# A four-layer graph network on one core: GpSimd's score tiles get a second ALU stage, and the planner a shorter price for them

## The chip, the cores and the metric

One Trainium2 chip, one of its cores. The metric is the device time of one execution in microseconds (us); the kernel before took 5291.05 us (median of three runs, 5291.04 to 5301.35). The engines are TensorE (PE), VectorE (DVE), ScalarE (ACT), GpSimd (POOL) and SyncE (SP, which here only issues DMAs). Each works through its own list of instructions in order[...].

## The reference

The input `x` is 64 graphs of 256 nodes with 128 features, `adj` one 256 x 256 matrix for all of them, everything in float32. Four layers follow each other; each normalizes, clips at zero, and adds its result to `x`:

```python
h = jnp.maximum(_layernorm(x), 0.0); x = x + _L0(h, adj, adj, ...)   # 5 steps of a gated recurrence
h = jnp.maximum(_layernorm(x), 0.0); x = x + _L1(h, adj, adj, ...)   # Chebyshev hops of order 2
h = jnp.maximum(_layernorm(x), 0.0); x = x + _L2(h, adj, ...)        # product, rows scaled to length 1
h = jnp.maximum(_layernorm(x), 0.0); x = x + _L3(h, adj, ...)        # additive attention
```

The change lies in the last layer. Its scores need every pair of nodes (i, j) and every one of 256 features e:

```python
pre = s1[:, :, None, :] + s2[:, None, :, :] + b_lin
h = jnp.where(pre >= 0, pre, ALPHA * pre)          # ALPHA = 0.2
e = jnp.einsum('bije,e->bij', h, a) + bias
out = sigmoid(einsum('bij,bjf->bif', softmax(e, axis=2), x))
```

## The kernel before, in words

**Tiling.** Two graphs make a pair; there are 32 pairs. For each pair a *front* computes layers 0 to 2 and the two terms `s1` and `s2` of layer 3, as a chain of steps on PE, ACT, DVE and POOL. Then come the *scores* of the pair. Features lie on the 128 partitions in two halves (half 0: features 0 to 127, half 1: the others). A score tile `rl` holds 4 rows i, both graphs and all 256 j of one half (128 x 2048 numbers). 64 tiles per half and pair make 4096 tiles in all. Up to a part that is linear in `pre` and is added later (`lin`), leaky ReLU is a ReLU, and the ReLU of `s1 + s2` is `s1` minus the minimum of `s1` and `-s2`; what is constant along j drops out of the softmax, so a tile can be made in either form, and the weights `win` (for a ReLU) or `win_n` (for a minimum) carry the sign.

**Three makers of tiles** (`work_on_tile`):
- DVE makes half 0 only, one minimum of 128 x 2048 per tile (line 737), reading `s1a` from SBUF and `-s2` from a PSUM bank.
- ACT makes half 1 in 8 ReLU activations of 128 x 256 (line 750) from a PSUM copy of `s2n`, and takes a tile of half 0 (from `s2c` in SBUF) when DVE has fallen two tiles behind (`half`, `LAG`).
- POOL makes half 1 only, in 8 `tensor_scalar` instructions of 128 x 256 (line 757): the minimum of `s2n` with one column of `s1b`, a scalar for each partition. Two of these are one part of a tile, and a tile has four parts.

PE then multiplies each tile with `win` or `win_n` into one of two score banks (`score`, line 794: four column groups of 32, which the trace shows as 8 matmuls, two passes each). After 64 tiles of both halves a block of 128 rows i is done, and a *tail* makes the softmax and the output: `lin` is added on POOL (line 648), the exponential on ACT (line 656), and `o = 0.5 o + 0.5` on POOL with an immediate `mult` and an immediate `add` (line 686), followed by the addition of `x3` (line 687).

**The order.** It is planned while the program is built. `clock[engine]` is the planner's time for each engine; `ran(engine, us, ...)` books a piece of work with a price written in the code, and the loop at the end takes the engine that is earliest and gives it, of what is ready by the plan, a step of a tail first, then of a front, then a tile. The prices for tiles are 2.2 us on DVE, 1.43 us (half 1) or 1.6 us (half 0) for 4 activations on ACT, 1.8 us for two instructions on POOL, and 0.86 us for the matmuls of a tile. `in_order` then fixes each engine's list. The plan thus decides who makes which tile and where each tile stands in PE's list; the chip keeps the list, whatever the pieces really take. Thirteen `rl` buffers exist, of which DVE may hold 8, ACT 3 and POOL 2 (`MOST`); a buffer comes free when PE has multiplied its tile. A front's pace is set by the number of tiles scored (`chain_ready`), not by time, so fronts advance with the scores; the last front is through when 3920 of 4096 tiles are scored.

Of the kernel before, what the change touches and what calls it, by code (L numbers as in the profile page):

```python
# [10 lines left out]
OP = mybir.AluOpType  # L11
# [6 lines left out]
LN_EPS = 1e-5  # L18
NORM_EPS = 1e-12
ALPHA = 0.2  # L20
PE, DVE, ACT, POOL = ENGINES = (mybir.EngineType.PE, mybir.EngineType.DVE, mybir.EngineType.Activation, mybir.EngineType.Pool)
SLOTS = 64

# [2 lines left out]
def kernel(  # L26
# [50 lines left out]
    nc = tc.nc  # L77
# [22 lines left out]
    def ran(engine, us, *after):  # L100
        start = max(clock[engine], 0.0, *after)
        if engine == ACT:
            behind[0] = max(0.0, behind[0] - (start - clock[ACT])) + 0.024 * us
        clock[engine] = start + us
        return clock[engine] + SEEN[engine] + (behind[0] if engine == ACT else 0.0)
# [19 lines left out]
    last, done = {}, [0]  # L125
# [123 lines left out]
    def other_constants():  # L249
# [29 lines left out]
        for k in range(NE):  # L279
            nc.vector.tensor_scalar(win[:, k, 31:32], acol[:, k:k + 1], 1.0 - ALPHA, None, op0=OP.mult)  # L280
            nc.vector.tensor_scalar(win_n[:, k, 31:32], acol[:, k:k + 1], ALPHA - 1.0, None, op0=OP.mult)
            nc.vector.tensor_scalar(a_rep[:, k, :], a_rep[:, k, :], acol[:, k:k + 1], None, op0=OP.mult)
# [7 lines left out]
        yield DVE, t  # L290
        nc.vector.tensor_scalar(g2, b[0][:, 0:P], ALPHA, None, op0=OP.mult)
        t = ran(DVE, 0.25, t)
# [413 lines left out]
    def where(n):  # L706
        return n // SLOTS, n % SLOTS // 32, n % 32

    def half(e):

        return 0 if e == DVE or e == ACT and following[0] <= following[1] - LAG else 1

    def tile_ready(e):

        if e in begun:
            return 0.0
        n = following[half(e)]
        if n >= NSLOT or n // SLOTS not in READY or held[e] == MOST[e] or not tiles:
            return None
        return max(READY[n // SLOTS]["since"][half(e)], min(t[1] for t in tiles))  # L720

    def work_on_tile(e):
        if e not in begun:
            k = half(e)
            tiles.sort(key=lambda t: t[1])
            begun[e] = [following[k], k, *tiles.pop(0), 0]
            following[k] += 1
            held[e] += 1
        n, k, t, free, part = begun[e]
        p, ic, r = where(n)  # L730
        ops = READY[p]
        i0 = ic * P + r
        since = max(ops["since"][k], free)
        if e == DVE:
            whole = [P, 4, NB, N]
            rows = ops["s1"][0][:, :, i0:i0 + 97:32].rearrange("p b g -> p g b").unsqueeze(3)
            nc.vector.tensor_tensor(t, rows.to_broadcast(whole), ops["s2a"].unsqueeze(1).to_broadcast(whole), op=OP.min)  # L737
            done = ran(DVE, 2.2, since)
            t_s2v[p % 2] = done
            parts = 1  # L740
        elif e == ACT:
            if k and "s2p" not in ops:
                ops["s2p"] = s2p
                nc.scalar.copy(s2p, ops["s2n"])
                ran(ACT, COPY, since)
            parts = 2
            for g in (2 * part, 2 * part + 1):
                for b in range(NB):
                    i = i0 + g * 32
                    nc.scalar.activation(t[:, g, b, :], (s2p if k else ops["s2c"])[:, b, :], AF.Relu,  # L750
                                         bias=ops["s1"][k][:, b, i:i + 1], scale=-1.0)
            done = ran(ACT, 1.43 if k else 1.6, since)
        else:
            parts = 4
            for b in range(NB):
                i = i0 + part * 32
                nc.gpsimd.tensor_scalar(t[:, part, b, :], ops["s2n"][:, b, :], ops["s1"][1][:, b, i:i + 1], None, op0=OP.min)  # L757
            done = ran(POOL, 1.8, since)
        begun[e][4] += 1
        if part + 1 == parts:  # L760
            del begun[e]
            made.append((done, n, k, t, e))
# [55 lines left out]
    def chain_ready(key, e):  # L818

        engine, since, bank, gate = (*CHAINS[key][1], 0, None)[:4] if len(CHAINS[key][1]) < 4 else CHAINS[key][1]  # L820
        if engine != e or bank and not spare or gate and not gate():
            return None
        if not isinstance(key, tuple) and 0 < key < NPAIR and spare:

            due = STEPS_OF_FRONT * (scored[0] / (2 * SLOTS) - (key - 2)) / SPREAD
            if CHAINS[key][2] > due + AHEAD:
                return None
        return max(since, min(b[1] for b in spare)) if bank else since
# [15 lines left out]
    while scored[0] < 2 * NSLOT or CHAINS:  # L844
# [4 lines left out]
        for key in CHAINS:  # L849
            since = chain_ready(key, e)  # L850
# [6 lines left out]
        else:  # L857
            since = tile_ready(e)
# [3 lines left out]
        if ready:  # L862
            _, (rank, *_), what = min(ready, key=lambda x: x[1])
            if rank < 2:
                advance(what)
            elif e == PE:
                score(what)
            else:
                work_on_tile(e)
            in_order()  # L870
            now[e] = max(now[e], clock[e])
        else:
            later = [x[0] for x in todo] + [t for t in now.values() if t > now[e]]
            now[e] = min(later) if later else now[e] + 1.0
# [31 lines left out]
```

## Time and profile before

| what | value |
|---|---|
| runs of the kernel | 5301.35, 5291.04, 5291.05 us; median 5291.05 us |
| span of the profiled execution | 5298.6 us; the page gives it no other time, and of the runs the one of 5301.35 us is the nearest above it |
| granted TensorE clock | full, but for the first and the last stretch (0.96 and 0.90) |
| first score matmul | 123.3 us |
| last front's last ACT step (`s1a`, line 628) | starts at 5097.5 us |
| last score tile's matmuls | start at 5285.8 us |
| DMA | 7 GB/s on the mean |

How to read it: the page gives busy time as the union of an engine's instructions. The mean duration of a group can be longer than the distance between two starts, since instructions of an engine overlap at their ends; how fast a row really goes is read from a run of them in the timeline, or from its busy time divided by its count. PE's ends are modelled, so its busy share says little by itself. "Idle before" a row and the name after the arrow say how long the engine stood still and what ended that. In the table by stretches each engine's busy time is followed by the number of its instructions.

### The profile page before, as it was taken

How to read it: one execution, taken by the hardware profiler on the slowest of the kernel's cores; microseconds unless marked ns; L12 is line 12 of the kernel's file. 1: busy time of each engine (PE TensorE's matmuls, PEld its weight loads, DVE VectorE, ACT ScalarE, POOL GpSimd, SP SyncE). 2: the span in 40 equal slices, each digit the busy share in tenths (PEclk: the TensorE clock that was granted, in tenths of full speed). 3: DMA queues.
4: the chain of work that ended last, by engine and by line, in shares of the span. 5: the costliest groups of instructions: out<-in, count | busy, mean ns of one | idle time of the engine just before them, and what ended most of it. 6: DMA issues, size and time to landing. Idle time of an engine off the chain costs nothing. (4 is left out here: it accounts for less than half of the span.)

```text
span 5298.6 us, 138351 instructions
## 1 busy us (share of the span) xinstructions
PE 5215.3 (98%) x56085; PEld 1855.4 (35%) x56085; DVE 5194.6 (98%) x4198; ACT 5093.4 (96%) x13353; POOL 5126.0 (97%) x5894
## 2 busy tenths in 40 slices
PE   7999999999999999999999999999999999999998
PEld 3333333333333333333333333333333333333322
DVE  3999999999999999999999999999999999999999
ACT  4999999999999999999999999999999999999999
POOL 2999999999999999999999999999999999999998
PEclk9999999999999999999999999999999999999999
DMA  0000000000000000000000000000000000000000
GB/s 20 7 8 5 8 7 6 8 5 8 8 5 8 7 6 8 7 6 8 5 8 8 5 8 6 6 8 7 6 8 5 8 7 6 8 5 6 6 5 4
DMA packets 60338, 37.44 MB, mean 7 GB/s; under 512 B 4528, under 2 KB 59696, under 8 KB 59696
## 3 DMA queue, kind: packets, MB, share of 16 engines
q1 hardware_dynamic: 58976, 28.59, 2.3%
q8 instruction: 438, 7.18, 0.6%
q14 instruction: 204, 1.67, 0.1%
q10 hardware_dynamic: 720, 0.00, 0.0%
HBM read 18.09 MB, written 10.49 MB: 5 GB/s over the span
## 5 line engine op out<-in xcount | busy, mean ns | idle before, releaser
L757 POOL TENSOR_SCALAR rl<-s2n,s1b 128x256 f32<-128x256 f32 x5064 | 4565.0, 943 | 11.4 <-ACT s1b L619 8.9
L737 DVE TENSOR_TENSOR rl<-s1a,bank 128x2048 f32<-128x2048 f32 x2046 | 4545.1, 2276 | 10.6 <-ACT s1a L628 10.6
L750 ACT ACTIVATE rl<-bank,s1b 128x256 f32<-128x256 f32 x11320 | 4538.6, 923 | 2.5 <-PE bank L794 1.3
L794 PE MATMUL bank<-rl,win_n 128*32 128x512 f32 x21432 | 2646.6, 593 | 32.0 <-DVE rl L737 29.7
L794 PE MATMUL bank<-rl,win 128*32 128x512 f32 x11336 | 1493.5, 593 | 0.0
L794 PEld LDWEIGHTS bank<-rl,win_n 128*32 128x32 f32 x21432 | 678.2, 110 | 1513.5 <-issue 1242.2
L794 PEld LDWEIGHTS bank<-rl,win 128*32 128x32 f32 x11336 | 363.8, 110 | 745.6 <-issue 621.4
L305 PE MATMUL bank<-mT,wts 128*32 128x512 f32 x2560 | 332.9, 592 | 0.0
L305 PE MATMUL bank<-adj_t,h 128*32 128x256 f32 x5120 | 309.4, 382 | 3.6 <-ACT h L492 3.3
L473 POOL TENSOR_TENSOR d<-d,hT 128x512 f32<-128x512 f32 x155 | 203.3, 1311 | 53.2 <-ACT d L469 53.2
L305 PEld LDWEIGHTS bank<-adj_t,h 128*32 128x32 f32 x5120 | 165.4, 111 | 178.6 <-issue 63.1
L376 ACT ACTIVATE h<-x,mv 128x128 f32<-128x128 f32 x384 | 171.8, 631 | 45.3 <-POOL mv L372 45.2
L382 ACT COPY mT<-bank 128x512 f32<-128x512 f32 x160 | 149.0, 931 | 44.1 <-issue 21.8
L457 ACT ACTIVATE bank<-bank,gate_b 128x512 f32<-128x512 f32 x160 | 167.0, 1044 | 19.5 <-PE bank L305 19.5
L469 ACT ACTIVATE d<-bank,gate_b 128x512 f32<-128x512 f32 x155 | 166.7, 1076 | 7.3 <-PE bank L305 7.3
L305 PE MATMUL bank<-hT,wts 128*32 128x512 f32 x1280 | 167.3, 593 | 0.0
L305 PE MATMUL bank<-mT,w 128*32 128x512 f32 x1280 | 166.7, 593 | 0.0
L305 PE MATMUL bank<-rh,u5t 128*32 128x512 f32 x1280 | 166.6, 592 | 0.0
L434 ACT ACTIVATE bank<-bank,gate_b 128x512 f32<-128x512 f32 x160 | 152.9, 955 | 13.4 <-PE bank L305 12.8
L492 ACT COPY h<-bank 128x512 f32<-128x512 f32 x128 | 131.3, 1026 | 24.2 <-PE bank L333 21.2
L305 PEld LDWEIGHTS bank<-mT,wts 128*32 128x32 f32 x2560 | 82.3, 110 | 192.6 <-issue 154.9
L300 POOL TENSOR_TENSOR mv<-mv,minus_half 128x4 f32<-128x4 f32 x128 | 133.3, 1041 | 10.7
(118 smaller groups left out, 3088.7 us busy)
## 6 DMA issues: line engine op xcount, KB each, us to landing
xin<-in_x_dram SPq DMA_DIRECT2D x64, 128.0 KB, 2.2
lin<-row SPq DMA_DIRECT2D x32, 256.0 KB, 7.5
out_dram<-o SPq DMA_DIRECT2D x64, 128.0 KB, 1.8
row<-quarter SPq DMA_DIRECT2D x32, 64.0 KB, 1.5
w_raw<-in_L_gnn_w_w_dram SPq DMA_DIRECT2D x3, 128.0 KB, 2.5
th_raw<-in_L_gnn_Theta_dram SPq DMA_DIRECT2D x1, 320.0 KB, 3.9
adj_n<-in_adj_dram SPq DMA_DIRECT2D x1, 256.0 KB, 3.1
w_raw<-in_L_gnn_u_w_dram SPq DMA_DIRECT2D x2, 64.0 KB, 2.8
```

The costliest lines, as they stand in the source:

```text
L300: nc.gpsimd.tensor_tensor(t, t, minus_half, op=OP.pow)
L305: nc.tensor.matmul(o[g:g + 32], w[:, g:g + 32], t, start=start, stop=stop, skip_group_check=True)
L376: nc.scalar.activation(h[:, k, :], s[:, k, :], AF.Relu, bias=mv[:, k, 0:1], scale=mv[:, k, 1:2])
L382: nc.scalar.copy(c, by_feature(bank[0]))
L434: nc.scalar.activation(r[0], pr[0], AF.Tanh, bias=br, scale=0.5)
L457: nc.scalar.activation(pr[0], pr[0], AF.Tanh, bias=bz, scale=0.5)
L469: nc.scalar.activation(d, by_feature(pv[0]), AF.Tanh, bias=bh, scale=1.0)
L473: nc.gpsimd.tensor_sub(d, d, hT)
L737: nc.vector.tensor_tensor(t, rows.to_broadcast(whole), ops["s2a"].unsqueeze(1).to_broadcast(whole), op=OP.min)
L750: nc.scalar.activation(t[:, g, b, :], (s2p if k else ops["s2c"])[:, b, :], AF.Relu, bias=ops["s1"][k][:, b, i:i + 1], scale=-1.0)
L757: nc.gpsimd.tensor_scalar(t[:, part, b, :], ops["s2n"][:, b, :], ops["s1"][1][:, b, i:i + 1], None, op0=OP.min)
L794: nc.tensor.matmul(pe[g * 32:(g + 1) * 32, :], w[:, k, 31 - r:63 - r], flat(t[:, g]), start=first, stop=(left[block] == 0), skip_group_che ...
```

## The change

The minimum gets a second stage in the same instruction: the maximum with the lowest finite float32 number, which leaves every finite value as it is. Number, sources and targets of one tile's instructions stay: eight for each tile, of 128 x 256. The planner's price for two of them becomes 0.9 in place of 1.8.

```diff
@@ -18,6 +18,7 @@
 ALPHA = 0.2
+LEAST = -3.4028234663852886e38
@@ -754,8 +755,9 @@
             parts = 4
             for b in range(NB):
                 i = i0 + part * 32
-                nc.gpsimd.tensor_scalar(t[:, part, b, :], ops["s2n"][:, b, :], ops["s1"][1][:, b, i:i + 1], None, op0=OP.min)
-            done = ran(POOL, 1.8, since)
+                nc.gpsimd.tensor_scalar(t[:, part, b, :], ops["s2n"][:, b, :], ops["s1"][1][:, b, i:i + 1], LEAST,
+                                        op0=OP.min, op1=OP.max)
+            done = ran(POOL, 0.9, since)
```

Since the price enters the plan, the built program differs beyond this line. Counted in the two built programs, the tiles are shared out like this (half 0 and half 1 of ACT apart), by their place in PE's list:

| tiles, in PE's order | DVE | ACT half 1 | ACT half 0 | POOL |
|---|---|---|---|---|
| before, 1 to 3920 | 1960 | 1351 | 2 | 607 |
| after, 1 to 3920 | 1953 | 1158 | 7 | 802 |
| before, 3921 to 4096 | 86 | 64 | 0 | 26 |
| after, 3921 to 4096 | 75 | 43 | 13 | 45 |
| before, all | 2046 | 1415 | 2 | 633 |
| after, all | 2028 | 1201 | 20 | 847 |

In the middle of the run a pair of 128 tiles is split 64 DVE, 44 ACT, 20 POOL before, and 64, 38, 26 after. What ACT, after the last `s1a`, still has to do for tiles is 496 activations before, and 424 after (104 of them half 0). Matmuls, fronts, tails and DMAs are the same in number; before the first score tile PE's list holds the same 559 matmuls.

## The prediction

> **What bounds the kernel now.** First the busy shares, which only say that no engine rests:
>
> ```profile
> PE 5215.3 (98%) x56085; PEld 1855.4 (35%) x56085; DVE 5194.6 (98%) x4198; ACT 5093.4 (96%) x13353; POOL 5126.0 (97%) x5894
> ```
>
> Then the table by stretches (length, then busy time of PE, PEld, DVE, ACT, POOL), cut where the last front ends (5097.5 us) and where the last tile's matmuls start (5286 us):
>
> ```profile
> 130.00:5097.50 4967.50, 4935.33 (x53456) 1759.33 (x53450) 4955.04 (x3969) 4848.05 (x12732) 4916.32 (x5647) 1.00 0.03 7
> 5097.50:5286.00 188.50, 172.39 (x1495) 52.60 (x1491) 186.49 (x91) 187.32 (x513) 184.11 (x207) 1.00 0.01 3
> ```
>
> In the long stretch DVE stands still for 4967.5 - 4955.0 = 12.5 us, 0.25%; POOL for 51, ACT for 119. PE's ends are modelled, so I summed its starts instead: distances beyond the cadence of the form (a tile's 8 matmuls take 0.86 us back to back) come to some 65 us between 200 and 5000 us. PE has 1.3% of slack, and DVE practically none. In the second stretch no front is left; three makers are full and PE waits. The waits of DVE in the first stretch confirm that nothing holds it up (us, times, longest):
>
> ```profile
> DVE bank L476 <- POOL d L473: 2.3, 7, 0.6
> DVE x L568 <- POOL rn L300: 0.6, 2, 0.3
> DVE nmx L652 <- POOL sc L648: 0.4, 1, 0.4
> ```
>
> So **DVE sets the pace until the last front is through, the three makers together after that**. The head (to 123 us, one pair's chain with no tiles yet) and the last tail (5286 to 5298.6) are chains without POOL tiles.
>
> Last, the price of POOL's instruction. The groups and the rows by line (duration min/median/max):
>
> ```profile
> L757 POOL TENSOR_SCALAR rl<-s2n,s1b 128x256 f32<-128x256 f32 x5064 | 4565.0, 943 | 11.4 <-ACT s1b L619 8.9
> L737 DVE TENSOR_TENSOR rl<-s1a,bank 128x2048 f32<-128x2048 f32 x2046 | 4545.1, 2276 | 10.6 <-ACT s1a L628 10.6
> ```
>
> ```profile
> L686 POOL TENSOR_SCALAR o<-o x63: 407/407/483, 228.5 to 5253.7; 128x256 f32<-128x256 f32 x63
> ```
>
> ```profile
> 2507.22 23.37 POOL L757 TENSOR_SCALAR rl<-s2n,s1b 128x256 f32<-128x256 f32 x26
> ```
>
> The one-stage minimum takes 943 ns, 23.37 / 26 = 0.90 us from start to start. The two-stage `mult`, `add` of line 686 has the same operation and shape and takes 407 ns. More work in less than half the time: the one-stage instruction is not limited by its arithmetic.
>
> [...] Line 737 has one input in SBUF and one in PSUM, and its starts in a row lie 2.20 us apart throughout (5th to 95th percentile 2.194 to 2.198) beside a POOL that is 97% busy: [...] I charge DVE nothing for a faster POOL.
>
> **The change part by part.**
>
> *The instruction.* Not in the trace: a `min`, `max` pair with one scalar from SBUF. Lower bound 0.37 us (407 ns less the 45 ns by which starts lie closer than durations in line 757)[...]. I take **0.45**: the two-stage row [...]. What decides for the low end: both instructions are TENSOR_SCALAR on unit-stride float32, and the missing second stage is the plainest difference; but pointer against immediate, and min/max against mult/add, differ too, and no row separates them.
>
> *POOL's load.* 847 tiles x 8 = 6776 instructions x 0.45 = 3049 us, plus its other work 5126.0 - 4565.0 = 561: 3610 us, 69% of the span. POOL no longer limits. A pair takes 162.4 us (3920 tiles in 4972 us, times 128) and holds 26 POOL tiles; POOL would be the limit from (162.4 - 561/32) / 208 = **0.70 us** per instruction.
>
> *The plan, up to the last front.* POOL takes over 195 tiles (607 to 802), nearly all from ACT (1353 to 1165). DVE's share stays at 64 in every middle pair, because POOL can make only half 1: the engine that sets the pace is relieved of only 1960 - 1953 = 7 tiles x 2.20 = 15.4 us. PE's slack of 65 us covers that. The 12.5 us of DVE's idleness can shrink a little, since `d`, `rn` and `lin` come from an idler POOL. A few of the 7 tiles may lie where PE is the later one. I take **-12 us**.
>
> *After the last front.* DVE 86 to 75 tiles: 11 x 2.20 = 24 us less. ACT: before, 499 instructions in 186.3 us, 0.373 each. After, 320 at 0.373 and 104 on half 0; those read SBUF and start 0.40 us apart, against 0.36 for half 1, so 0.415: 119.4 + 43.2 = 162.6, 24 less. PE's floor: 176 tiles x 0.86 = 151 plus 4.8 for the tails' matmuls (busy time there), 156. POOL: 45 x 8 x 0.45 = 162 plus 6 for the tails, 168, 20 less than 188.5. The latest of four now nearly equal limits sets the end; I take **-22 us**. This part hangs on the instruction: at 0.50 POOL needs 186 us and the gain is gone; at 0.40 it needs 150, and ACT and DVE decide.
>
> *Head, last tail, DMAs, waits.* The same 559 matmuls come before the first tile, and the same chain after the last: 0. The DMAs stay the same in number, at 7 GB/s. Added waits are for free buffers (DVE 574 wait instructions against 503, 21 ns each, 1.5 us in all; ACT 613 against 360, 17 ns each, 4 us beside ACT's new slack of some 600 us). Behind a DVE wait stand its own chain steps; but the plan prices a DVE tile at 2.20 and chain steps at 0.61 where the chip needs 0.68, so DVE trails the plan and its buffers are free before it comes. Cost 0 here; if that cover fails, see the second rival.
>
> Sum: -12 - 22 = **-34 us**: span 5298.6 to about 5265, the median 5291 to **5257 us** (the median lies 7.6 us under the profiled span; I carry the difference over). Hard floor: all 18 DVE tiles (39.6 us) and all its idleness in the first stretch give -52, about 5239.
>
> **Rivals.**
>
> 1. *The instruction keeps its slow form* (the scalar in SBUF, or the minimum, is the reason). The plan hands POOL 847 tiles on a false price: 6776 x 0.90 = 6098 + 561, plus the 173 us that POOL stands idle now: about 6830 us of span, **6820 us**. PE would wait for POOL in every pair. For it: line 757 is the only row with such a scalar. Against it: [...]the excess over line 686 is 0.5 us. It decides from 0.70 us per instruction[...].
> 2. *The gain is eaten in the long stretch.* The new order puts DVE behind buffers or behind ACT's steps: 1 us per pair is 30 us. **5290 us.** For it: PE has only 1.3% of slack and everything is in fixed order. Against it: DVE's waits there are 3.6 us in 30 pairs, and ACT and POOL, on which it waited, get idler.
> 3. *PE takes over fully*: all DVE savings count and idleness vanishes, **5239 us**. Against it: half 0 stays with DVE.
>
> **How the numbers follow.** What a measurement of this kernel can tell from no change is about 0.2%, 10.6 us. My forecast (5240 to 5280) gets 0.73; rival 1 0.14; rival 2 (5280 to 5300) 0.10; rival 3 0.03. Faster: 0.73 + 0.03 less 0.02 near the bound, 0.74; within 0.2%: 0.02 + 0.08, 0.10; slower: 0.14 + 0.02 of rival 2, 0.16. The range takes the forecast and rival 2, from 5238 to 5300; it leaves out rival 1.
>
> **What would show it.** Right: POOL's row at 0.40 to 0.50 us per instruction and POOL near 70%; DVE still within 20 us of full in the long stretch with ACT some 700 us below it (4848 less 188 tiles x 3.2); the last front through some 12 us earlier, and the stretch after it near 166 us. Wrong: POOL's row above 0.7 us and PE waiting for it; DVE waits above 30 us in the long stretch; or a last stretch that is still 180 us or more because POOL or ACT fills it.

## The result and the profile after

The kernel after takes **5241.66 us** (median of four runs, 5241.6 to 5242.4) against 5291.05 us before (four runs): -49.4 us, a ratio of 0.9904 with a 95% interval of 0.989 to 0.9919. The forecast was 5257 us, -34 us.

Busy shares and the chain that ended last, of the kernel after:

```profile
span 5239.9 us, 138951 instructions
PE 5197.2 (99%) x56085; PEld 1856.9 (35%) x56085; DVE 5140.0 (98%) x4180; ACT 4563.7 (87%) x11785; POOL 3635.0 (69%) x7606
...
PE 92%; ACT 5%; DVE 2%; issue 0%; POOL 0%; DMA 0%; ACTq 0%; POOLq 0%
```

Of four full engines two are left: POOL fell from 97% to 69% and ACT from 96% to 87%, and the chain is PE's for 92% of the span. In the kernel before the page follows the chain over the last 16% of the span only, and there it runs through DVE, PE and POOL in turns:

```profile
DVE 6%; PE 5%; POOL 3%; issue 1%; ACT 1%; POOLq 0%; ACTq 0%; DVEq 0%
```

A large share of the chain on PE does not mean that DVE has room; the table further down shows that it has next to none.

GpSimd's row, and a run of 96 of its instructions in the timeline (start, length, count at the end):

```profile
L758 POOL TENSOR_SCALAR rl<-s2n,s1b 128x256 f32<-128x256 f32 x6776 | 3057.5, 475 | 1025.1 <-PE bank L796 994.9
```

```profile
5063.93 43.05 POOL L758 TENSOR_SCALAR rl<-s2n,s1b 128x256 f32<-128x256 f32 x96
```

43.05 / 96 = 0.448 us from start to start, half of the 0.90 before; POOL now waits 995 us for buffers that PE frees.

The table by stretches, cut as before where the last front's `s1a` starts (5064.0 us) and the last tile's matmuls start (5227.5 us); columns are length, then PE, PEld, DVE, ACT, POOL:

```profile
130.00:5064.00 4934.00, 4928.79 (x53476) 1761.51 (x53473) 4926.44 (x3963) 4342.41 (x11238) 3448.61 (x7203) 1.00 0.03 7
5064.00:5227.50 163.50, 160.60 (x1463) 51.24 (x1455) 160.30 (x78) 163.14 (x438) 160.73 (x354) 1.00 0.01 3
```

The long stretch is 33.5 us shorter and the last one 25.0. In the long stretch DVE stands still for 7.6 us in place of 12.5, and PE, by its modelled busy time, for 5 us in place of 32. ACT has 590 us of room there, POOL 1485.

One caution on spans: the span of 5298.6 us of the kernel before belongs to an execution of about 5300.3 us (the time lies 1.7 to 1.9 us above the span in the runs that give both), while most of its executions take 5290 to 5293 us. The difference of the spans, 58.7 us, is thus some 9 us more than that of the medians. The experiments below split the gain by medians.

One row of DVE, not a POOL one, changed without having been edited: the negation of the mean in `norm`, a `tensor_scalar` of 128 x 4 with its own duration min/median/max, before and then after:

```profile
L368 DVE TENSOR_SCALAR mv<-mv x128: 169/258/1849, 4.8 to 5071.3; 128x4 f32<-128x4 f32 x128
```

```profile
L369 DVE TENSOR_SCALAR mv<-mv x128: 170/171/509, 4.7 to 5037.4; 128x4 f32<-128x4 f32 x128
```

The timeline of before around the longest shows what runs on POOL beside it:

```profile
2890.31 1.85 DVE L368 TENSOR_SCALAR mv<-mv 128x4 f32<-128x4 f32 x1
...
2890.81 1.32 POOL L648 TENSOR_TENSOR sc<-sc,lin 128x512 f32<-128x512 f32 x1
```

DVE's small instruction ends at 2892.16, 30 ns after POOL's addition (2892.13). The three others of over a microsecond (1582, 1343 and 1186 ns) end with an addition of POOL's line 648 in the same way. Of the 87 instances over 200 ns before, 37 end within 35 ns after the end of one of POOL's instructions; the others do not line up with an end (28 of them end 0.47 us after one). In the kernel after, all 34 over 200 ns end within 45 ns after one.

### The profile page after: what moved, and what is told of

Its sections match the earlier page's. It is cut to its first block, busy times and chain, and to the rows that moved or that the text cites. A ratio compares the mean times of both kernels' runs of the same rounds, so it can differ in the third digit from the quotient of the medians.

```text
span 5239.9 us, 138951 instructions
## 1 busy us (share of the span) xinstructions
PE 5197.2 (99%) x56085; PEld 1856.9 (35%) x56085; DVE 5140.0 (98%) x4180; ACT 4563.7 (87%) x11785; POOL 3635.0 (69%) x7606
## 4 chain that ended last, share of the span: by engine, by line
PE 92%; ACT 5%; DVE 2%; issue 0%; POOL 0%; DMA 0%; ACTq 0%; POOLq 0%
PE bank L796 61%; PE bank L306 27%; ACT rl L751 5%; PE bank L334 2%; DVE rl L738 2%; PE bank L327 1%; POOL rl L758 0%; PE bank L595 0%; DVE hT L481 0%; DVE stats L366 0%; ACT h L493 0%; DMA xin<-in_x_dram 0%; DVE bank L477 0%; DVE x L569 0%; POOL mv L301 0%
## 5 line engine op out<-in xcount | busy, mean ns | idle before, releaser
L751 ACT ACTIVATE rl<-bank,s1b 128x256 f32<-128x256 f32 x9608 | 3691.7, 605 | 139.0 <-PE bank L796 137.9
L758 POOL TENSOR_SCALAR rl<-s2n,s1b 128x256 f32<-128x256 f32 x6776 | 3057.5, 475 | 1025.1 <-PE bank L796 994.9
L796 PE MATMUL bank<-rl,win_n 128*32 128x512 f32 x23000 | 2764.7, 593 | 6.2 <-DVE rl L738 6.0
L796 PE MATMUL bank<-rl,win 128*32 128x512 f32 x9768 | 1282.5, 593 | 0.0
L796 PEld LDWEIGHTS bank<-rl,win_n 128*32 128x32 f32 x23000 | 735.1, 110 | 1543.1 <-issue 1297.6
L796 PEld LDWEIGHTS bank<-rl,win 128*32 128x32 f32 x9768 | 307.0, 110 | 656.3 <-issue 620.7
L383 ACT COPY mT<-bank 128x512 f32<-128x512 f32 x160 | 101.0, 631 | 99.4 <-PE bank L306 59.7
L657 ACT ACTIVATE sc<-sc,nmx 128x256 f32<-128x256 f32 x128 | 59.5, 523 | 132.5 <-DVE nmx L653 132.5
L458 ACT ACTIVATE bank<-bank,gate_b 128x512 f32<-128x512 f32 x160 | 117.6, 735 | 44.2 <-PE bank L306 44.2
L435 ACT ACTIVATE bank<-bank,gate_b 128x512 f32<-128x512 f32 x160 | 118.8, 742 | 30.0 <-ACT rl L751 20.9
```

The source lines that it names most:

```text
L383: nc.scalar.copy(c, by_feature(bank[0]))
L435: nc.scalar.activation(r[0], pr[0], AF.Tanh, bias=br, scale=0.5)
L458: nc.scalar.activation(pr[0], pr[0], AF.Tanh, bias=bz, scale=0.5)
L796: nc.tensor.matmul(pe[g * 32:(g + 1) * 32, :], w[:, k, 31 - r:63 - r], flat(t[:, g]), start=first, stop=(left[block] == 0), skip_group_che ...
```

## The experiments

**The form alone.** In the kernel after, the old price brings the old order back; the instruction keeps its two stages.

```diff
-            done = ran(POOL, 0.9, since)
+            done = ran(POOL, 1.8, since)
```

> The two-stage instruction of the change in the old order (the planner's price stays 1.8 us, so DVE makes 2046 tiles, ACT 1417, POOL 633 as before). Theory (the gain comes from the tiles that the plan moves off DVE and ACT[...]): POOL's row about 474 ns, POOL near 54% busy; the long stretch up to the last front gains only what DVE loses less to POOL, 10 to 15 us; the last stretch stays near 188 us because ACT has the same 496 activations; 5275 to 5285 us in all. Rival (a faster POOL by itself frees the chains, the new shares are secondary): 5245 to 5255 us.

Measured: 5278.61 us (11 runs, 5277.9 to 5280.6) against 5290.7 for the kernel before on the same chip, ratio 0.9977 (0.9968 to 0.9986): -12.1 us. POOL is busy for 54%. By stretches:

```profile
130.00:5077.00 4947.00, 4927.60 (x53465) 1762.13 (x53468) 4938.87 (x3970) 4840.85 (x12736) 2756.78 (x5658) 1.00 0.03 7
5077.00:5265.00 188.00, 163.96 (x1488) 41.74 (x1484) 186.47 (x91) 187.77 (x515) 90.68 (x196) 1.00 0.01 3
```

The last stretch keeps its length, 188.0 us against 188.5, with POOL half idle in it: ACT's 496 activations and DVE's 84 tiles hold it. A faster POOL without the new shares brings nothing there. Nearly all of the 12 us lies in the long stretch, where DVE sets the pace. The theory held, and the rival fell.

**The price alone.** In the kernel before, the new price brings the new order; the instruction keeps its one stage.

```diff
-            done = ran(POOL, 1.8, since)
+            done = ran(POOL, 0.9, since)
```

> The new order (847 tiles on POOL) with the one-stage instruction. Theory (POOL sets the pace from 0.70 us per instruction): 6776 x 0.90 = 6098 us plus 561 of other work plus POOL's idle time of the kernel before, about 6820 us; PE waits for POOL's tiles in every pair. Rival (the fixed order has enough slack to hide part of it behind DVE and ACT): below 6400 us.

Measured: 7006.16 us (one run). The mechanism is that of the first rival of the prediction: POOL is busy for 6646.5 us of a span of 7004.4, and PE and its weight loads wait 267 and 756 us for POOL's tiles. The size is 2.7% over the estimate because POOL stood idle for 358 us and not for 173; 150 of them are waits for one of its two buffers, which only PE frees:

```profile
POOL rl L757 <- PE bank L794: 150.2, 29, 6.0
POOL d L473 <- ACT d L469: 80.7, 33, 16.2
```

The rival, a slack that hides part of it, fell.

**DVE's negation without a `tensor_scalar`**, in the kernel before:

```diff
-        nc.vector.tensor_scalar(mv[:, :, 0], mv[:, :, 0], -1.0, None, op0=OP.mult)
+        nc.vector.tensor_reduce(mv[:, :, 0], mv[:, :, 0:1], AX.X, OP.add, negate=True)
```

> The kernel before, with DVE's negation of the mean (tensor_scalar, 128 x 4, 128 times) done by a tensor_reduce with negate over one element. Theory (that tensor_scalar waits for POOL's instruction in flight: 349 ns on the mean and up to 1849 before, 212 ns after the change, about 0.2 us from start to start against 0.12; DVE sets the pace): the row falls to 0.12 us or less with no long ones, and the time by some 8 to 10 us, to 5281 to 5284 us. Rival (the longer rows are noise of the profile, or DVE does not set the pace): no change, 5288 to 5292 us.

Measured: 5283.52 us (21 runs), ratio 0.9986 (0.9979 to 0.9992): -7.2 us, just short of the 8 to 10. The row no longer has long instances, though POOL is 97% busy beside it as before:

```profile
L368 DVE TENSOR_REDUCE mv<-mv x128: 157/157/161, 5.0 to 5055.1; 128x4 f32<-128x4 f32 x128
```

With this instruction the longest instance falls from 1849 ns to 161 and the time by 7.2 us: the long instances were no noise of the profile, and DVE did set the pace. The rival fell.

**A dearer DVE in the plan of the kernel after.** DVE gives up 164 of 2028 tiles.

```diff
-            done = ran(DVE, 2.2, since)
+            done = ran(DVE, 2.4, since)
```

> The kernel after, with the planner's price of a DVE tile at 2.4 us in place of 2.2; DVE then makes 1864 tiles in place of 2028 (361 us of work less), ACT 184 of half 0 and POOL about 962 tiles. If DVE still sets the pace after the change, the time falls until another engine binds, by over 40 us to about 5195. If PE now sets the pace (its distances beyond its own cadence sum to some 41 us between 130 and 5064 us), it falls by 0 to 25 us, 5215 to 5242. If the shares no longer fit the real speeds of ACT and POOL, it rises.

Measured: 5231.92 us (5231.4 to 5233.3), 9.7 us below the kernel after (timed for the result above and not beside it), ratio to before 0.9889 (0.9876 to 0.9903). 361 us of work less on DVE bring 10 us, the case expected if PE sets the pace. PE stands right behind DVE in the kernel after, and here it is the limit:

```profile
130.00:5049.80 4919.80, 4919.80 (x53508) 1767.30 (x53504) 4630.50 (x3804) 4540.64 (x11726) 3808.80 (x8008) 1.00 0.03 7
```

PE, by its modelled ends, is busy for the whole of the stretch; DVE has 289 us of room. The long stretch is 14.2 us shorter than in the kernel after, and the one from the last `s1a` to the last tile some 6 us longer. DVE's negation again has long instances (up to 1476 ns, 48.8 us in all). This is the fastest version measured here.

**The kernel before once more**, unchanged, on another chip than the first set.

> The kernel before, unchanged, profiled once more: the profiled execution of before was the slowest of its runs, 5301.35 us against 5290 to 5293 us of all others. Theory (it lost some 10 us to DVE's tensor_scalar of line 368, whose longest instance took 1849 ns): a span near 5289 us, line 368 with less than 44.7 us busy. Rival: line 368 is the same, and the 10 us lie elsewhere in DVE's or PE's rows.

Measured: 5299.67 us, span 5297.9, and 5298.9 to 5300.7 in nine further runs on that chip. The theory of a span near 5289 could not be decided where the kernel takes 5299 anyway. Line 368 has 42.7 us busy there and a longest instance of 1774 ns, nearly those of the first profile. The kernel before thus takes 5290.7 us in the median on two chips and 5299.3 on a third, but one of 33 executions on one of the two took 5301.53 us, so the longer time is not bound to the chip. Form and reduce together (below), the one version run on both kinds of chip, differs by 0.4 us. No profile of an execution at 5290 exists, and what makes these 9 us stays open. Longer instances of line 368 would fit: from the profile of before to that of the reduce, DVE's time for the row, summed from start to start, falls by 16.7 us (34.7 to 18.0), while the medians fall by 7.2.

**Another second stage.** The sum with 0.0 in place of the maximum.

```diff
-                nc.gpsimd.tensor_scalar(..., LEAST, op0=OP.min, op1=OP.max)
+                nc.gpsimd.tensor_scalar(..., 0.0, op0=OP.min, op1=OP.add)
```

> The kernel after with an addition of 0.0 as the second stage in place of the maximum. Theory (any second stage takes the instruction out of its slow form): POOL's row within 20 ns of 474 ns and 5241 us. Rival (the pair of minimum and maximum is a special case): a row near 940 ns and, as POOL then limits, about 7000 us.

Measured: 8425.94 us (one run). My theory fell, and the rival had the row too short (940 ns) and the time too:

```profile
L758 POOL TENSOR_SCALAR rl<-s2n,s1b 128x256 f32<-128x256 f32 x6776 | 7590.2, 1146 | 107.9 <-PE bank L796 99.4
```

A second stage as such does not make the instruction short: with the addition it takes 1.12 us from start to start, against 0.90 with one stage. With the maximum it took 0.448.

**One stage with immediates.** In the kernel after, the tails' `mult`, `add` is split.

```diff
-        e.tensor_scalar(o, o, 0.5, 0.5, op0=OP.mult, op1=OP.add)
+        e.tensor_scalar(o, o, 0.5, None, op0=OP.mult)
+        e.tensor_scalar(o, o, 0.5, None, op0=OP.add)
```

> The kernel after with the tails' two-stage instruction (mult, add, 405 ns, both immediates, 128 x 256) split into two one-stage instructions with immediates. Theory (the missing second stage is what makes an instruction slow, not the scalar in SBUF and not the minimum): each takes 850 to 960 ns, and the time rises by less than 10 us since POOL has room. Rival 1 (the scalar in SBUF is the reason): each takes about 405 ns or less. Rival 2 (the minimum is): the same, 405 ns or less.

Measured: 5245.02 us (one run, on the chip where the kernel before takes 5299), the two rows at 872 and 862 ns on the mean, where the fused one had 405. Both one-stage rows, neither with a scalar in SBUF nor with a minimum, stand near the 943 ns of the one-stage minimum in the tiles of before and not near 405; both rivals fell.

**Nine forms beside each other**, added to every tail but the last of the kernel after, each into a tile that nothing reads (lines 689 to 697):

```diff
+        if not end:
+            scr = work.tile([P, NB, D], F32, name="scr")
+            e.tensor_scalar(scr, o, 0.25, None, op0=OP.min)
+            e.tensor_scalar(scr, o, 0.25, LEAST, op0=OP.min, op1=OP.max)
+            e.tensor_scalar(scr, o, 0.25, 0.5, op0=OP.max, op1=OP.min)
+            e.tensor_scalar(scr, o, 0.25, 0.0, op0=OP.min, op1=OP.add)
+            e.tensor_scalar(scr, o, 0.25, 1.0, op0=OP.min, op1=OP.mult)
+            e.tensor_scalar(scr, o, 0.25, 0.5, op0=OP.add, op1=OP.mult)
+            e.tensor_scalar(scr, o, 0.25, 0.5, op0=OP.add, op1=OP.max)
+            e.tensor_scalar(scr, o, rs[:, 0:1], 0.5, op0=OP.mult, op1=OP.add)
+            e.tensor_scalar(scr, o, rs[:, 0:1], None, op0=OP.mult)
```

> The kernel after with nine more GpSimd tensor_scalar instructions of 128 x 256 in every tail but the last, each into a scratch tile that nothing reads: min alone; min, max; max, min; min, add; min, mult; add, mult; add, max (all with immediates); mult, add and mult alone with a scalar from SBUF. Theory ([...] mult, add at 405 ns and min, max at 474 ns are known to be short, min, add at 1144 ns long; kind and place of the scalar do not matter): mult, add with the SBUF scalar near 440 ns, min, max with immediates near 405; one-stage rows 850 to 950; the others 1050 to 1150 ns unless they belong to the short ones (max, min and add, mult are the open cases). Rival (the SBUF scalar has a form of its own): mult, add with the SBUF scalar over 850 ns.

Measured: 5270.83 us (one run), and these groups (mean ns after the comma):

```profile
L695 POOL TENSOR_SCALAR scr<-o 128x256 f32<-128x256 f32 x63 | 68.3, 1085 | 5.2
L692 POOL TENSOR_SCALAR scr<-o 128x256 f32<-128x256 f32 x63 | 68.2, 1082 | 5.2
L691 POOL TENSOR_SCALAR scr<-o 128x256 f32<-128x256 f32 x63 | 67.6, 1073 | 5.3
L693 POOL TENSOR_SCALAR scr<-o 128x256 f32<-128x256 f32 x63 | 67.6, 1073 | 5.2
L697 POOL TENSOR_SCALAR scr<-o,rs 128x256 f32<-128x256 f32 x63 | 58.8, 933 | 6.2
L689 POOL TENSOR_SCALAR scr<-o 128x256 f32<-128x256 f32 x63 | 54.1, 859 | 39.3 <-ACT o L682 38.9
...
L696 POOL TENSOR_SCALAR scr<-o,rs 128x256 f32<-128x256 f32 x63 | 30.4, 483 | 6.2
...
L694 POOL TENSOR_SCALAR scr<-o 128x256 f32<-128x256 f32 x63 | 25.6, 407 | 5.2
L690 POOL TENSOR_SCALAR scr<-o 128x256 f32<-128x256 f32 x63 | 25.3, 402 | 5.4
```

Three pairs are short: min, max (402 ns), add, mult (407) and mult, add (407, the tails' own). Four are long: max, min; min, mult (1073 each); min, add (1082); add, max (1085). One stage lies between (859 for min with an immediate, 933 for mult with a scalar from SBUF). Min, max took 402 ns and max, min 1073, but their constants differ too (`LEAST` as the second against 0.5), so whether the order of the two counts is not shown. With a scalar from SBUF a row took some 60 to 85 ns more, the short ones (483 against 407; 475 in the tiles against 402) as the long ones (933 against the 872 of the one-stage `mult` above; 943 in the tiles of before against 859). The theory held but for this difference, and the rival fell. Why just these pairs are short is not shown.

**Form and reduce together**, first on the third chip:

> The two-stage instruction in the old order (5278.6 us) with DVE's negation by tensor_reduce as well. Theory (both gains, 12.1 us of the form and 7.2 us of the reduce in the kernel before, are mostly the same thing, DVE waiting for POOL's instruction in flight): 0 to 4 us below form_alone, 5274.5 to 5279 us. Rival (two independent gains): 7 us below it, 5271 to 5272 us.

Measured: 5276.61 us (five runs), 22.7 us below the kernel before of that chip, 5299.3. `form_alone` had run on another chip, so the set was repeated on one chip, where the kernel before takes 5290.77:

> form_alone once more, on one chip with the two below: the kernel before took 5290.7 us on the chip of the first set and 5299.3 on that of the second. Theory (most of the form's gain is DVE no longer waiting for POOL's instruction in flight): 12 to 20 us below the kernel before of the same chip, 5278 to 5281.

> form_and_reduce on the same chip. Theory (form and reduce remove the same wait of DVE): 0 to 4 us below form_alone_2. Rival (two independent gains): 7 us or more below it.

> before_negate_by_reduce on the same chip: 7 us below the kernel before where that takes 5290.7 us, up to 15 us below it where that takes 5299; within 6 us above form_alone_2, what is left being DVE's waits for POOL's chain steps.

Measured there: the form alone 5278.96 (-11.8; ratio 0.9977, 0.9968 to 0.9986), the reduce alone 5283.18 (-7.6; 0.9986, 0.9980 to 0.9993), both 5276.24 (-14.5; 0.9972, 0.9961 to 0.9984). Independent gains would sum to 19.4 us; with the form in place the reduce brings 2.7 us and not 7.6. The intervals are 3 to 6 us wide on each side, so this rests on the runs of the one set, which lie apart: 5278.4 to 5279.5 with the form, 5274.7 to 5278.1 with both (resampled, they leave the overlap of the two gains between 2.8 and 6.2 us). So 4.9 of the form's 11.8 us are the reduce's gain under another name, line 368 without its long instances (310 ns at most with the form, 1849 in the trace of before); 6.9 remain when the reduce stands on both sides (14.5 - 7.6). My theory that this is most of the form's gain is thus not borne out on this chip: it is two fifths.

The rest is what the last expectation named, DVE's waits for POOL's chain steps. In the long stretch, with the reduce alone:

```profile
DVE bank L476 <- POOL d L473: 1.6, 4, 0.6
DVE x L568 <- POOL rn L300: 0.9, 3, 0.4
DVE nmx L652 <- POOL sc L648: 0.6, 2, 0.5
```

With the form as well, the same list holds no wait for POOL. It leaves short waits out; summed from DVE's starts, what comes before these three steps takes 6.3 us less, of the 8.4 by which DVE's starts in these two profiles differ. The tiles are not what changes: where one tile follows another, 1407 times, it takes 2.197 us in both profiles, as in those of before and of the form alone.

## Why the prediction was right, and where it was short

*The instruction* (forecast 0.45 us, measured 0.448). The number was right by luck, and the reason was not right. I took 407 ns for the pair and, as an estimate that no row of before gave, 40 for the scalar; measured are 402 and 73, less 27 ns by which the starts lie closer than the durations, and the errors cancel. I called the missing second stage the plainest difference between the two rows; but with an addition as the second stage the instruction gets longer (1.12 us). Of the seven pairs tried three took 402 to 407 ns and four 1073 to 1085; that min, max would be among the three, no row of before could tell. The scalar in SBUF, on which the first rival stood, made a difference of 61 to 84 ns. What a wrong guess about the pair costs, the addition shows: 1.12 us and 8426 us.

*POOL's load* (69%, measured 69%) and the limit of 0.70 us per instruction: the two runs beyond it, at 0.90 and 1.12 us, made POOL the bound, as it said. That DVE, not POOL or PE, sets the pace before was right: shortening one small row of DVE brought 7 us.

*The plan up to the last front* (forecast -12 us). From the form alone to the kernel after the last front ends 13.0 us earlier (5077.0 to 5064.0). Right: summed from its starts, DVE's tiles up to there take 13.1 us less, six of them fewer by that time. The negation takes 4.6 us more than with the form alone, and other steps give about as much back.

*After the last front* (forecast -22 us, to 166 us). From 188.0 to 163.5 us: -24.5. DVE, ACT and POOL are each busy for 160 to 163 of these 163.5 us, the balance of nearly equal limits that was worked out; POOL's 0.448 us was just short enough.

*"I charge DVE nothing for a faster POOL"*: this is the step that failed. The form alone brought 12.1 us, where the sum had only a little less idleness of DVE. I had looked at line 737 only, and for it the reading holds (2.197 us from tile to tile beside either POOL); but I carried it over to DVE as a whole. Line 368 is a `tensor_scalar` from SBUF to SBUF. In the trace of before it takes 258 ns in the median and 1849 at most, for 4 numbers per partition, and the four longest end with an instruction of POOL; but the row was too small to be noticed. The added time is part of the instruction's own duration and shows in no list of waits: DVE's list for the long stretch of before has 3.6 us in all and none at line 368. In the two profiles it takes DVE 34.7 us from start to start before and 20.4 with the form alone; by the medians of one chip it is 4.9 of the form's 11.8 us. The rest are DVE's waits for POOL's `d`, `rn` and `sc`. The prediction saw these, but let them "shrink a little" within its -12 us; they are worth some 7.

The measured parts are -12.1 us (the form alone), -13.0 and -24.5. That they add up to the -49.4 measured is bookkeeping, not a test. Of the 15 us that the forecast of -34 lacks, 12 are the form alone.

*Waits in the new order* (forecast 0): right: the list has 0.3 us of waits of DVE in the long stretch after the change; the second rival did not come. The third rival, PE taking over, came in part: PE is the chain for 92%, but DVE is full beside it; a plan that frees DVE further gains 10 us, and PE is then busy without a gap.

## What to carry to other kernels

When all engines look full, ask which of them would be relieved: a faster helper pays mostly through what the planner then moves off the engines that set the pace (37 of 49 us here), and a wrong price in a static plan costs far more (1715 us here) than a right one brings (37 us). When an operation's time is doubtful, put the candidate forms into one run beside each other: what looked like "one more stage is faster" holds for three of seven pairs (402 to 407 ns against 859 to 872 with one stage) and is the reverse for the others (1073 to 1085). And read the rare long instances of small rows on the engine that sets the pace: here they went up to 1849 ns, stood in no list of waits, and another instruction for the row brought 7 us.

## What was not expected of the hardware

GpSimd's `tensor_scalar` on 128 x 256 float32 came at three prices here: 402 to 407 ns for the pairs min, max; add, mult; mult, add; 859 to 872 for one stage with an immediate; 1073 to 1085 for the other pairs tried, max, min among them. With a scalar from SBUF it took some 60 to 85 ns more. In the two runs where PE waited for POOL's tiles (267.4 and 827.8 us in the lists of waits), the granted TensorE clock was 0.941 (`price_alone`) and 0.907 (another second stage) against 0.997 to 0.999 in the others, though PE had the same matmuls in a longer span (7004.4 and 8424.2 us); no run here separates the cause.
